# An attention and FFN layer on one core: the first pair's weights are split twice and kept in the second row, and a multiply moves to GpSimd

## The chip, the core and the metric

The kernel runs on one core of a Trainium2 chip. A core has five engines that run side by side, each with its own queue of instructions in a fixed order: TensorE (PE, matmuls; its weight loads are listed as PEld), VectorE (DVE), ScalarE (ACT), GpSimd (POOL) and SyncE (SP, which here issues nearly all DMAs). An instruction waits at the head of its queue until what it needs is there, and everything behind it in that queue waits too. The metric is the device time of one execution in microseconds. Of the kernel before, three runs took 1340.47, 1340.90 and 1341.65 us; the median is 1340.9.

## The reference

The input is four sequences (rows of the batch, "rows" below) of 512 tokens with 512 features. One attention layer with 16 heads and one low-rank mixture FFN, each with a residual and a LayerNorm:

```python
q, k = heads(x @ Wq, 64), heads(x @ Wk, 64)
v = heads(x @ Wv, 128)
s = clip(heads(x @ Ws, 64), -32, 32)
z = cumlogsumexp(s, axis=time)
g, p = exp(z[t-1] - z[t]), exp(s - z)
hk = hk * g[:, None] + k[:, None] * p[None, :]      # for each step t
ok = q @ hk                                          # q scaled by 64 ** -0.5
pv = softmax(ok)
hv = hv * g[:, None] + p[:, None] * v[None, :]
ov = pv @ hv
o = ov * rsqrt(mean(ov ** 2) + 1e-5) * g_norm_weight
o = o * silu(x @ Wg)
x = layernorm(x + o @ Wo)
h = relu(x @ W1 + b1)
alpha = softmax(h @ W2 + b2)                         # 8 experts
x = layernorm(x + sum_k alpha[k] * U[k] @ (V[k] @ x))
```

## The kernel before

**Precision.** All matmuls take operands in a rounded 32-bit format (F32R). To keep float32 accuracy every operand is split into a high part (a copy that rounds) and a low part (the original minus the high part), and a product is three matmuls: high by high, high by low, low by high. So every weight and every activation costs one copy and one subtraction before PE can use it.

**Tiling.** Two heads make a pair; a row has eight pairs, p = 0 to 7, and a unit of work is one pair of one row, 32 in all. For each unit the steps are: `decay` (ps_s, and from it et, the running sum cum, its reciprocal rc, and est), `key` and `query` (ps_k, ps_q), `gates` (ps_g, gate), `value` (ps_v, vh, vl), two causal score steps over `attend` (PE writes pa; ACT copies it to `at`, DVE subtracts and adds, POOL masks it with an affine select), `sum_keys` (po_k), `soft` (a softmax of twelve small steps on DVE, ACT and POOL, which ends in wst), `sum_values` (po_v), `norm` and `combine` (po_y, added by DVE to the row's tile y). After its eight pairs a row goes through LayerNorm, the FFN (ps_h, pt_lg, ps_vx, po_f) and the second LayerNorm, between the attention units of the row that follows.

**The order.** A recording layer (`InOrder`) chains all instructions of all engines in program order, so each engine's queue holds its instructions in exactly the order in which the program calls them. That order comes from a long string, `PLAN`, written by a planner: a letter takes the next step of its kind and issues its PE work (s decay, k key, q query, g gates, v value, c and d the two score steps, x and y the two sums, o soft, n norm, w combine, b and f a weight fetch, and so on). A step leaves its work for other engines behind in small pieces, one list for each letter and engine. A mark and a letter issue the next such piece: `^` ACT, `.` DVE, `,` POOL, `;` SP; a number between them skips pieces. `SLOTS` are strings of digits, also from the planner, that say which of the buffers wt0 to wt6, wraw0 to wraw5, tmp0 to tmp6 and pa0 to pa3 each new tile takes.

**Weights.** `fetch(key, on)` brings one weight tile of 128x512. Its key is the matrix and the pair, with a half for g, v and o: a pair has nine (s, k, q, two g, two v, two o). The first fetch of a key, in the first row (letter b), loads the raw tile from DRAM into a `wraw` buffer, makes the high and the low part in a `wt` buffer, and stores both parts (512 KB) to a scratch tensor in DRAM, `kept_...`. Each later fetch of the key (letter f) reads that tensor in one DMA. High and low part are made by ACT and DVE; for pair 0 and the matrices s, k, q, g and v POOL makes both (`early`).

**The norm.** `norm(u, h, on)` takes one head. PE multiplies the split squares by a matrix of 1/128 (pt_ms); ACT computes Ln and Exp, which gives `rstd`, the reciprocal norm; DVE multiplies the gated value t1 by it in place (in the profile `t<-t,rstd`); ACT makes the high part oh and POOL the low part ol, and `combine` multiplies both by Wo. There are 64 of these.

Of the kernel before, what the change touches and what calls it, by code (L numbers as in the profile page):

```python
# [18 lines left out]
def tile_abc_attention_ffn(  # L19
# [22 lines left out]
    class InOrder:  # L42
# [41 lines left out]
        lpoooooooommoooooooooooooooooooooooorrrr,p,pbbbblbbl^l.ll^l.ll^l,b.l^l,b.ls,b;bb,1b^b,b.b^bq,b;bb.s  # L84
        ;1b.b^sb,b;bb.sek^q;b,sb.q^s,b^see.s^ke,s;b^kb^e.suuk^u^b,b.k,1b.e,b.ui.b^1k^i^i,b;bb.i.i;bb^i,ic^c
        ^c.c.1c^c;b,b.cb^k.c.cu,c^cs.k^b;p,c.c,b.c.b,c;bxb.cxx^b.s;b,cxbx.bx^sxxx.s,se;bxgb^s,s^x^s.x.sxx^ge
        ug.s^x^g.x^u,x^g.u^b.ge^g.oq^b.b^g.o;b^gb.b^o.g;bb.o^q.pv,o^b.q.b^oev^e.o;bb.e^oi^v.ov^i,o.v^i.i.i.o
        ^it,i^t.ov^t.t^o.t.o^bd^v.b^b.v;b^db.b^dg^d.d;b^d.1db.d.d,d.d,d.1d.dy^g.d,d^b,dy^g.by^g;b^yyb.g^yv
        ^1y.y^y.y.1yc,y.1y^c^c.y,y^cv.c^c.1c.yv^v.c.c,c.c,c.1cnxv.c^n.c,c.v^n,cx^b.nxxx^vx.bxxx^nx.vx;bx^xg
        ,nb^x.x^b.x.b,x;bsb^b.o.b.o;bb^o.s^s.ov,o^b.b,s^oeeee;bv.o^eb,s^o.et^v.o^t,o.v^t^g.tk.t^g.o^g.s.o^s  # L90
        .g^o^s.od^k.s^k^b.s^d.k^dq.d^d^d.1d.d.d,d.d,d.1d.du.du,d^qy.b^u,dy^b.q;byb^y.u.b^yy;b.yi^ybs.y^y^i,y
        .1y^i.1y.y.iv.i^b.s^i.b,i^sc;b.s,sb^c^c.c^sk.1c,s^c.c^s.c.c^c,c.s,c.cv.s^k,c^k.c^b.kxe^bxex.c^vux.b
        ,cxexx.vx^x;bnxb.b^n,yxxxt.x^n;bb.y^xv^t.n^t.x^nuq.t^u,x.t.u,n.o.oew^q^o.qw^e.o.w,o.ew^o.w.og^o.w.o
        ,o.op^gwb.o^p^g.pv^o.w;p^g.o^b.gd^v.b^b.v^d;b^db.dg^d.1d^d.d^b.d,d.d,d.1d.d.d,di.b^gy,d^i^g.by;bb^i
        ^gy.i;b^y.iy.gb^i^y,ink^1y.y^y.y^n.1y,y^n.1y.yc^1k.n^c^n.c^ks.c,nl^c.k^c.c^c,c.1c.c.c,c.cp,c.sxvb^p
        .c^b.p,c^sl.b;p^b,st.s;b^lbx,sv^t^t.l^su.tx^vx.tnx.b^sx,ynx^n.vx;bexbv.y^n.s^x.nxxxv.s^n.x^x,n.xp^vu
        vb,x^p.v^u.p^bv.o^b;p^b.u.o^be.bq^v^o.b;bb.v^b;b.ob^b.b,ow.b;b^qb^oeg.q;bb.o.w^o.b^b.o;bewb.b^e,o.b
        ;b^bbg^n.o^g;bb.e^n^g.o.n^gw^o.w^g.gw^g.o^n.w^g.wd,n.g^d^d.d^d.1ds^d.d.d,d.d,d.1d.d.d,d.bi,d^iy.s^i
        ;bby.i^s.it^i.s,s^1yy^t^t.ty^s.t,i^yg,s^s.y^y.s^y.y.s,y.1yc^g.y^c^g.yk^c.c^g.1c^c.c^c.g,c.c.c,cx.1cp
        ^k.cx^kb.c,c^p.kuex^b,cx.pxx^bee.bx;px^xxx.bv^b;bb.x^b;b^b.bbxxn^b.bv;b,y^xb.b;b^nbg^n.y;bb^v.x.n,x  # L100
        .v^n.bq^g,n^g.o;bb^g.o.g^ow^q.o,o.qw.w^o.onu.we^ow^u.o^e.uv,o^n.w.e^nn.ov^1n.n^1n.op^v.nwb^o.v^p.o^n
        .p^n,n.wd;p^b^d.b,n^dk^d.d;b^d.1db^b.d.d,d^b.d^b,d.1d.di.d^1k,dy.b^i^i,dy.i;b.i^ib.by^y,i.by;b^ybs.y
        ;b^yb.y^y.1y,y.1y.y,yc.s^c.y^s.c^kg.s,s^c^c^c.k^s,s.c.c^s.1cq^g.s,c^g.c^g.s,c.c.cp,c^q.gepb^px.cebx
        ^px.q,cxx^bx.pxex^xnx.p;px^bxux.x^nt.b^xl^n.b;bgb^t.x^t;p^l.n,x^b;b.t.t^b.lb^b.bw^g.o^b;bb^g.bw.o^b
        ;bb^g.wu^on.bw.g^u;bb.o.w,ov.u.w^ov.b^b.o;bb.b^ow.b;b^vb.o^ng;b.v,ob^b.w^n,n.o^n.b^bs.o^g;bb.n^g.b^o
        ^n.o;bb^ge,nw.s^e.g^s.e^b.s.wd^d^d,s^s.d^d,s.1dg^s.d.d^d.s,d.d.s,d.di.d^g,dy.b^i^gy.d;b^i,d^g.iyb.i
        ^i.gy^y,i^yv^1y.y^y.y.1yc,y.1y^c^c.y,y^cq.c^c.1c.y.c.c,c.c,cp.1c^qv.cb^p.c,c.q^b,c.p^bxxx.bx^v;pexx
        ^bx.bxxe^xx.vxx;b^bl;b.xn^xbee.b^lbw.x^n;bb.l^e,xfk^n.w.n.o.el.o^kfg.b^k^o.k;bb^l.o,o.lv^o^b.o.bu^ou
        t;b^u.ovb^t.u^t,o^g.t.t^gi.ow^v.o^g.v^i^ow.g^i.o^nf.i,n^b.i.w^i.wd^d^d,i.d^d^d.1ds.d.d,d.d,d.1d.d.d
        ,d.b,dy^b.s;byb.b^st^1y;b.s,sy^t^ty.t^s.t,sk^y^s.y^y.s^y.y.s,y^1kf.1yc^c.y^c.y^kg^c.c^c.k.c.c,c.1c.c  # L110
        v.c^gf,c.c^g,c.ce,ce^gxxxn.gxx^nx,yxxex^x.yxn^nxx.xev^x.n^e.x^nqf.e^v,xf.v,n.o.on^qwf^o.qu.ov.w,o^ow
        .o^ow.w.ou,oq.w^u^n.u.o^2n^n.o^1n.n^ow.nf.o^nf.wd^nf,n^d^d.d,n^d.1dv^d.d.d,d.d,di.1d^vy.d^i.d,d^i.v
        ,dy.i.i^iy,i^y^yy.ys^y.y^y,y.1y.1y.y,yc^b.s^c.y^s.c^ck.s,s^q^c^c.q^s,s.c.c^s.1cg^k.s,c^k^b.c.s,c.c.c
        xt,c^gf.k^txe^g.cxx.b,cxv^t^g.t;b.t.bux.gx;bx^xxnx.xx^nexv^x^n.xef.ne^vv,xf^e.v.ew.o.ow.w^o.ouv.w,o
        ^u.u^og^v.o.v^o.o,ov^gf^g.oi^g.ow^i.g^i^o.i.iw.o^i,i.w^nf.wdf,n^d^d.d^d.1ds^d.d.d,d.d,d.1d.d.d,dy,d
        .sfy^st^1y.s,s^ty^t.tv^s.t,s^y^s.yy^b.sk^v.y^y.s^y,y.v^b.y.yc^1kf.y^c.b^c^k.cg;b^c.1c^c.k.c.c,c.c,c
        .1cv^gf.c.c,c^g.b,cx^gxux;bee.gnxx^nu,yxxxe^ux.y^nxxx.uv^x.n^x.x^ne.xg^v,n^e.v.e,xw.o^gf.o^gv^o.w^g
        .mw.g.o,oi.w^iq^i.m^o.i.o^m^m.m^o.mwf.i^q.o^i.q,om.wm^2m,i.og^2m.m.o^o.3m.ow^gf.3m^gf^g.wdf.g^d^d.m
        ^dv.d^d.d^m.d^m,dg^b.mf^v.m.d.d,d.1d.d.d,dm.v^gfy,d^m.bm^gy.m;b^mn^g.my^y.gy^yk^n.y^y.y^n,y^y.n.y^nf
        .yc^1k,n^c.y^c^ks^c.k^c.c.1c.c.c,c.cnqf,c.1cb.c,y.c.s,c.y,c^s.sxx,s^qexexxt.q^sx,sg^n^s^n.s^t.n^t^x  # L120
        .su^nxefx.th^g.t,n.x^g^g.gxx^hxw^h^b,hex.w^ev^x.b.e;bnhb.x^n,x^n.n.on^hw.o^hf^1n,hw.w^o^1n.nuv^u.w^b
        .o.u,ow.b^v^nfg.v^o;b,nb^n.w.o,n^oh.o^gf,o^g^g.o.gw^hf.o^hw^o.w^b.oi.bm^i^i.w;bw^m,h.i.i^i,i.wd^d^d
        .d^d.1dh^d.d.d,d.d,d.1d.d.d,dy,d^hfm^hy.m,hm^yy.m^yy.ym.y^yk^y.m,y.1y.y.ym^1k,yf.mc.y^c^c^k.cs^m.1c
        ^c.k^c.m.c.c,c.cnqf,c.1c.c.c,c.s,c^s.s,sxx^qxfmv.q^m^s,s.m^nxxv^s^n.s.nmf^vxfee.sx^mumx.v^xxh^1m.xxx
        .mufx^ut^x.ue^mh.x^t.m^t,x.t.t.ogf.m.o^m^o.m.om,of^om.m.om^o.m.ow.m,o^nf.oe^gvf,n^e.w^g.ov^g.e^o.gn
        ^vm.o^n.vf^n.mdf.n^d^d.d^n.1dh^d.d,n^d.d.d.1d,d.d.d,dm,dyf^m,dt.m^ti^my^t.m^iy^i^y.t.ty^y.i.i^ig.y^y
        ,i.y^y.1y,y.1y.y,yc^gf^g.y^c^gs.c^c.g^c.c^c.c,c.1c.cx.cm,cf.ch,c.s.c^s,c.s,sxxfxx^sexx,s^mxk^s.m^x.s
        ^m.x.sn.m^kxfxxv^k^n.k^nux.nee^xm.x,xn.mmm^1n.1m^1n.oeg^e.n.o.m^o.eu.omf^u,o.m.u^ow.2m^m^m.ov.m^o.m
        ;m.w;mmmmmf.o^vf.1m,o^gf.v^gwf.o^g.mg.o.g^o.w.ow.m^gf^gw^m.w^g^mf.g^nf^n.wd,n.m^d^d,n^dq.d^d;m.1d.d
        .d,d.d,d.1d.dy.d,d^qf.mi,d.q^iy;m^i.iy.i^y^iy^y,is^1y.y^y.y.1y,y.1yl.y,yc.s^c.y^s.cf^ck,s.s^c^c,s.c  # L130
        ^s.c.1c^svf.c,c^k.s^k,c.cv.s,c.cn.k^vxxex.c^nux.vx,cex^nxxxx^xx.next^x.x^te.xu^tq^e.t,x.t^u.e.u.o.ov
        ^qf^o.qi.o,o^iw^i.i.i^i^o,iw.w.ow^o.w.ow.w,o^nf.onvf,n^n.w^n.osf^v.nf^o.v^n.o,nd.sf^s^d.s,s^dg^d^d.d
        ^s.1d,s.d^s.d.d,d.sv^gf,d^g.d.sl,d^gy.d^l.gv.d.l,dy^vy.v^y^yy.yv^y.y^y,y.1yw.1y.y,y.wc.y^c^c.c^ck.1c
        ^c.c.c,c.c,c.1c.c.c,cxl^kf,cxx^kn^l.kxxux^nx.lxex^xxex^nx.xt^x.ne^ten^t.xq^e.t,x.t.e.o.ow^qf^o.quv.o
        ^u.w,o.ugf^of^v.o.v^o^1n.ow,o^gf^1n.o^gg.n^g.o.g^o.ww.o^gf^gf^n.wdf^n,n^g^d.gg,n^d.d^d^d.1d.d.d,d.d
        ,d.1dl.d^gf.dy,d^ll,d^g.li^ly^g.ly^i.g^i^yy.i^y.is^i.y^y,i.y^y.1y,y.1yw.yf,y.s.yv^s.w,s.s,sc^c^s.ck
        ^c.c^s,c.c^c.s^c.c.s,c.cev^kf.1c^k.c.c,c.kxx,c^vxxxen.vex^nnxxx^xv^n.x^1n.nx^1nxxt^x.n^tuu.xw^t^u.t
        ,x.t.uv.w.owf.o^vf^o.vw.w.o^nf,oeq.w^nf,n^e^o.e.o,n^ogf^q.o,o.q.ow^gf.o^gv^o.w^g.o.gd^d^d.d^d.1ds^d
        .d.d,d.d,d.1d.d.d,dy,d.sfv^s.s,si^vy^i.v^sy,s^i^s.iy.i^i.s^yk,i^y.s^1y.y^y.y.1y,yc^1kf.1y.y^c,y^c.c
        ^kq.1c^c.y^c.k.c.c,c.c,cv.1c^qf.c.c,c.qx,cxnxx^nxexxx^nuxx^xxe.neut^u.x^tx.ug^t^x.t.t.x,xw^gf.o^g.ow  # L140
        ^g.w^o.gv.o.w,osf^of^v.o.v^o.owf,o^nf.ovf,n.w.oev^e.s^o.e^sg.o^v.s.v^s^sdf^g.s^d.s^g,s.dg^d^g.d,s.d
        ^d.g^d,d.d.d,d.1di^gf.dv.d^i,d^g,d^i^g.iy.i^i.gy,iy^y^yy.yv^y.y^y,y.1yfc^vf.1y^c.y^c.v^ck^c.c.1c.c.c
        ,c.c,c.1cn.c^kvf.c,c^k^n,y.kn,c^n.yexxx^1nxux.nx^1nv^x.n^n.xxe^v,nt^t.vxex^tx.txx.tg^x.x,xuw.o^gf^u
        .o^g.uw^o.w^g.mv.g.o.w,ov.m^owf^m.of^v^m.v^onq.m^1n.m.o^1n.w,o.m.om^qfem^2m.og^e.n^o.q^2m.o.3mw.e^gf
        .3m^gf^n.wdf^n,n.m^g^d.gs,n^m^d.d^m.1d^d^d.m.m.d.d,dv.df,d.1d.d.dv,d.s,d^si.s,st^i^i^ty.i^t.i^s.ty,s
# [49 lines left out]
    def f(t):  # L195
# [8 lines left out]
            04152041520415364201543620136541362054120536  # L204
        """,
        "wraw": """
            0123450132450132450132450132450132450132450132450132450132450132450132450132450132450132514032514032
            5140325140325140325140404032
        """,
        "tmp": """  # L210
# [1175 lines left out]
```

## Time and profile before

| | |
|---|---|
| median of three runs | 1340.9 us |
| profiled execution, whole time | 1339.01 us |
| profiled execution, span from the first to the last instruction | 1337.3 us |
| mean granted clock of TensorE | 0.998 |
| PE busy | 1317.9 us, 8706 matmuls |
| DVE, ACT, POOL busy | 1084.5, 847.2, 553.5 us |
| DMA | 212.36 MB, 159 GB/s over the span |

The page comes from one profiled execution. A group's line names the engine, the operation, the tile written and the tiles read (buffer numbers left out), the shape and the count; after the bar stand the busy time in us, the mean duration of one in ns, and the idle time of the engine just before these instructions, with what ended it ("<-DVE at": an instruction of DVE that wrote `at`). PE's matmuls are pipelined: each is shown with a modelled end that overlaps the next. In a timeline the columns are start in us, duration in us, engine, line, operation, tiles, shapes and count, and in brackets the idle time before. L56 is the line of the recording layer through which nearly all instructions pass, so lines of the program can't be told apart by it, and the tiles' names are used.

### The profile page before, as it was taken

The numbers are of one execution on the slowest core, as the hardware profiler recorded it, in microseconds if no ns is written. First come the engines' busy times: TensorE is split into PE (matmuls) and PEld (weight loads), VectorE is DVE, ScalarE is ACT, GpSimd is POOL, SyncE is SP. The second block draws the span as 40 slices with busy tenths as digits, with TensorE's granted clock in tenths as the row PEclk, the third lists the DMA queues.
The fourth block names the chain that finished last, engine by engine and source line by source line (L and its number), as shares of the span: only waits on it lengthen the run. The fifth ranks groups of instructions, "written<-read, shape, count | busy, mean of one in ns | idle before, by whom it ended". The sixth has DMA issues, their size and how long they took to land.

```text
span 1337.3 us, 24043 instructions
## 1 busy us (share of the span) xinstructions
PE 1317.9 (99%) x8706; PEld 1139.0 (85%) x8706; DVE 1084.5 (81%) x2075; ACT 847.2 (63%) x1858; POOL 553.5 (41%) x623
## 2 busy tenths in 40 slices
PE   9999999999999999999999999999999999999997
PEld 7878888888888888888888888888888888888885
DVE  5888999988788778877779678878778887877855
ACT  4767787766676556666566655666666666666632
POOL 8344444444434343534343533334433344453310
PEclk9999999999999999999999999999999999999999
DMA  9555767763444346433344433544444343344452
GB/s 323 181 166 174 260 197 243 251 209 119 156 143 151 127 142 205 162 130 135 98 146 139 170 111 126 188 143 135 150 142 136 101 158 127 117 136 142 143 173 95
DMA packets 94007, 212.36 MB, mean 159 GB/s; under 512 B 12992, under 2 KB 43712, under 8 KB 93888
## 3 DMA queue, kind: packets, MB, share of 16 engines
q1 hardware_dynamic: 93360, 210.56, 46.9%
q8 instruction: 69, 1.13, 0.3%
q14 instruction: 50, 0.41, 0.1%
q10 hardware_dynamic: 528, 0.26, 0.1%
HBM read 162.55 MB, written 48.23 MB: 158 GB/s over the span
## 4 chain that ended last, share of the span: by engine, by line
PE 87%; DVE 7%; ACT 3%; POOL 1%; issue 1%; DMA 0%; SPq 0%; POOLq 0%; ACTq 0%; DVEq 0%
PE po_y L56 12%; PE ps_g L56 12%; PE ps_v L56 12%; PE po_v L56 7%; PE ps_s L56 6%; PE ps_k L56 6%; PE ps_q L56 6%; PE pa L56 5%; PE po_k L56 4%; PE ps_h L56 3%; PE po_f L56 3%; PE ps_vx L56 3%; PE pt_s L56 3%; PE pt_ms L56 1%; DVE at L56 1%
## 5 line engine op out<-in xcount | busy, mean ns | idle before, releaser
L56 POOL TENSOR_SCALAR_AFFINE_SELECT at<-at 128x512 fp32r<-128x512 f32 x256 | 170.8, 689 | 137.2 <-DVE at L56 123.3
L56 PE MATMUL po_y<-wt,oh 128*128 128x512 f32 x512 | 176.2, 396 | 0.1
L56 DVE TENSOR_TENSOR at<-pa,at 128x384 fp32r<-128x384 f32 x256 | 131.5, 549 | 7.4 <-ACT at L56 6.7
L56 POOL TENSOR_TENSOR ol<-t,oh 128x512 fp32r<-128x512 f32 x64 | 85.7, 1347 | 113.4 <-ACT oh L56 112.9
L56 ACT CAST at<-pa 128x384 fp32r<-128x384 f32 x256 | 107.5, 492 | 29.9 <-PE pa L56 28.2
L56 PEld LDWEIGHTS po_y<-wt,oh 128*128 128x128 f32 x512 | 96.3, 188 | 20.2 <-DVE okc L56 0.3
L56 PE MATMUL po_y<-wt,ol 128*128 128x512 f32 x256 | 100.2, 391 | 0.2 <-POOL ol L56 0.2
L56 DVE TENSOR_TENSOR y<-y,po_y 128x512 f32<-128x512 f32 x128 | 86.8, 680 | 11.6 <-PE po_y L56 10.7
L56 POOL TENSOR_SCALAR sqs<-sq 64x512 fp32r<-64x512 f32 x64 | 50.0, 781 | 95.1 <-DVE sq L56 84.0
L56 PE MATMUL po_v<-at,vh 128*128 128x256 f32 (+1 forms) x512 | 87.4, 278 | 0.0
L56 POOL TENSOR_TENSOR okc<-okc,rc 128x512 f32<-128x512 f32 x32 | 43.8, 1370 | 98.6 <-DVE okc L56 98.6
L56 PE MATMUL po_k<-at,ee 128*128 128x256 f32 (+3 forms) x512 | 82.9, 287 | 0.9 <-POOL at L56 0.8
L56 ACT ACTIVATE sq<-po_v 64x512 f32<-64x512 f32 x128 | 75.1, 591 | 9.5 <-PE po_v L56 7.5
L56 PEld LDWEIGHTS po_v<-at,vh 128*128 128x128 f32 x512 | 77.9, 190 | 0.9
L56 ACT ACTIVATE sg<-ps_g 128x512 f32<-128x512 f32 x64 | 38.2, 597 | 60.7 <-PE ps_g L56 55.7
L56 PEld LDWEIGHTS po_k<-at,ee 128*128 128x128 f32 (+1 forms) x512 | 69.0, 163 | 5.8 <-POOL at L56 2.1
L56 POOL TENSOR_TENSOR pr<-pr,mx 128x512 f32<-128x512 f32 x32 | 34.0, 1062 | 90.3 <-DVE mx L56 89.9
L56 POOL TENSOR_TENSOR pr<-pr,ss 128x512 f32<-128x512 f32 x32 | 33.9, 1059 | 88.5 <-DVE ss L56 62.4
L56 PE MATMUL po_v<-at,vl 128*128 128x256 f32 (+1 forms) x256 | 69.9, 273 | 0.3 <-POOL at L56 0.3
L56 DVE TENSOR_TENSOR at<-at,pa 128x128 fp32r<-128x128 f32 x256 | 62.8, 279 | 0.4
L56 DVE TENSOR_TENSOR t<-po_v,gate 128x512 f32<-128x512 f32 x64 | 44.1, 689 | 20.9 <-ACT sq L56 18.0
L56 POOL TENSOR_SCALAR est<-et 128x512 fp32r<-128x512 f32 x32 | 39.0, 1218 | 52.3 <-PE pa L56 23.7
(303 smaller groups left out, 3873.5 us busy)
## 6 DMA issues: line engine op xcount, KB each, us to landing
wt<-kept_v SPq DMA_DIRECT2D x48, 512.0 KB, 3.7
wt<-kept_g SPq DMA_DIRECT2D x48, 512.0 KB, 3.4
wt<-kept_o SPq DMA_DIRECT2D x48, 512.0 KB, 3.7
wt<-kept_s SPq DMA_DIRECT2D x24, 512.0 KB, 4.0
wt<-kept_k SPq DMA_DIRECT2D x24, 512.0 KB, 3.8
wt<-kept_q SPq DMA_DIRECT2D x24, 512.0 KB, 3.7
kept_g<-wt SPq DMA_DIRECT2D x16, 512.0 KB, 5.5
kept_v<-wt SPq DMA_DIRECT2D x16, 512.0 KB, 4.1
```

The costliest lines, as they stand in the source:

```text
L56: ins = fn(*args, **kwargs)
```

## The change

There are two changes, and a new `PLAN` and new `SLOTS` that order the whole program with them.

First, the nine keys of pair 0 (`key[1] == 0`, matrices s, k, q, g, v, o) are not kept in the first row: the split is made and used, and nothing is stored. In the second row the raw tile is loaded again and split again, then by ACT and DVE, and stored; the third and fourth rows read the kept tensor. All these second fetches count as first ones (letter b) in the lists that `PLAN` draws from. The DMA that loads a raw tile goes through ACT's queue for the very first fetch and through SP's for all others, as before; the test is on the new set `seen`.

Second, the multiply by the reciprocal norm is issued on POOL and not on DVE.

```diff
+    seen = set()
...
-        (SP if kept else ACT).dma_start(raw.rearrange("p (a b) -> p a b", a=a), src)
-        kept[key] = dpool.tile([P, 2, 512], F32, name="kept_" + "_".join(map(str, key)))
-        early = nm in "skqgv" and p0 == 0
+        (SP if seen else ACT).dma_start(raw.rearrange("p (a b) -> p a b", a=a), src)
+
+        again = key not in seen and key[1] == 0 and nm in "skqgvo"
+        seen.add(key)
+        if not again:
+            kept[key] = dpool.tile([P, 2, 512], F32, name="kept_" + "_".join(map(str, key)))
+        early = nm in "skqgv" and p0 == 0 and again
...
             (POOL if early else DVE).tensor_sub(wt[:, 1, :], raw, f(wt[:, 0, :]))
 
+        if again:
+            return
+
         @on("s")
         def _():
             SP.dma_start(kept[key], f(got[0]))
...
-        @on("d")
-        def _():
-            DVE.tensor_mul(t1, t1, j.pop("rstd"))
+        @on("p")
+        def _():
+            POOL.tensor_mul(t1, t1, j.pop("rstd"))
...
-    first = list(dict.fromkeys(key for key in wanted if key[0] not in "VU"))
-    later = list(wanted)
-    for key in first:
-        later.remove(key)
+    first, later = [], []
+    for i, key in enumerate(wanted):
+        n = wanted[:i].count(key) - (key[1] == 0 and key[0] in "skqgvo")
+        (first if n < 1 and key[0] not in "VU" else later).append(key)
```

The first two lines of the old `PLAN` and of the new one:

```diff
-        lpoooooooommoooooooooooooooooooooooorrrr,p,pbbbblbbl^l.ll^l.ll^l,b.l^l,b.ls,b;bb,1b^b,b.b^bq,b;bb.s
-        ;1b.b^sb,b;bb.sek^q;b,sb.q^s,b^see.s^ke,s;b^kb^e.suuk^u^b,b.k,1b.e,b.ui.b^1k^i^i,b;bb.i.i;bb^i,ic^c
...
+        lpoooooooommoooooooooooooooooooooooorrrr,p,pbbbbblbl^l.ll^l.ll^l,b.l^l,b.ls,bb,1b^b,b.b^bk,bb.s;bb.b
+        ^s,bb.se;b^kb,s^kuee.ke^suq,b^e^s.e^u,sb.s^bk,b^q.u.s,1b.q,b.bi^1k^i,bb^i.i;b.ib^i,ic^c.c^cb^c.c,b.c
...
```

## The prediction

> **What bounds the kernel now.** I read the page's busy shares first, then the busy time by stretch, then what TensorE (PE) waited for, then the rows of the instructions that the change moves.
>
> ```profile
> PE 1317.9 (99%) x8706; PEld 1139.0 (85%) x8706; DVE 1084.5 (81%) x2075; ACT 847.2 (63%) x1858; POOL 553.5 (41%) x623
> ...
> PE 87%; DVE 7%; ACT 3%; POOL 1%; issue 1%; DMA 0%; SPq 0%; POOLq 0%; ACTq 0%; DVEq 0%
> ```
>
> PE is the bound: it is busy for 99% of the span and carries 87% of the chain that ended last. A change that leaves PE's work alone can only win what PE still loses. Where that is, the stretches show (columns: length, then busy us and instructions of PE, PEld, DVE, ACT, POOL, then clock, DMA share, GB/s):
>
> ```profile
> 9.20:30.00 20.80, 18.93 (x103) 15.40 (x104) 15.26 (x26) 10.16 (x23) 18.03 (x18) 1.00 1.05 359
> 30.00:60.00 30.00, 28.99 (x217) 25.25 (x215) 25.07 (x48) 23.03 (x52) 9.86 (x13) 1.00 0.71 239
> 60.00:100.00 40.00, 37.02 (x259) 31.91 (x259) 35.08 (x68) 26.14 (x58) 18.83 (x20) 1.00 0.43 138
> 100.00:150.00 50.00, 50.00 (x367) 45.04 (x366) 45.52 (x85) 38.13 (x85) 23.03 (x25) 1.00 0.53 182
> 150.00:250.00 100.00, 99.11 (x639) 84.09 (x638) 94.52 (x176) 78.87 (x168) 46.19 (x47) 1.00 0.76 256
> 250.00:350.00 100.00, 99.52 (x703) 86.57 (x703) 84.75 (x167) 67.60 (x152) 42.81 (x48) 1.00 0.48 164
> ```
>
> PE idles 1.87, 1.01, 2.98, 0, 0.89 and 0.48 us: 7.2 us between 9.2 and 350 us, and from there to 1300 us the same view has only 1.5 us more. The other 11 us of idle time are the start and the tail, which the change does not touch. From 30 us on VectorE (DVE) is at 84 to 95% in these stretches: in the first row it splits weights besides its usual work. PE's waits from 9.2 to 100 us name it:
>
> ```profile
> PE pt_k L56 <- DVE at L56: 0.9, 1, 0.9
> PE ps_k L56 <- DVE vl L56: 0.9, 1, 0.9
> PE ps_v L56 <- DVE et L56: 0.8, 1, 0.8
> PE pt_k L56 <- ACT kf L56: 0.6, 1, 0.6
> ```
>
> **The change part by part.** The instruction orders of the two programs give the counts: PE 8708 in both, DMAs on SP 477 in both, DVE 2077 to 2022 (64 norm multiplies gone, 9 splits more), ACT 1861 to 1870, POOL 628 to 692. PE's matmuls are the same ones; the plan only shuffles them. Distances below are PE's own work between two places of an order, at 0.227 us for a 512-column matmul (ps_s x12 in 2.72 us in the timeline).
>
> ```profile
> L56 DVE TENSOR_TENSOR t<-t,rstd 128x512 f32<-128x512 f32 x64 | 47.9, 753 | 8.9 <-ACT rstd L56 8.1
> L56 POOL TENSOR_TENSOR okc<-okc,rc 128x512 f32<-128x512 f32 x32 | 43.8, 1370 | 98.6 <-DVE okc L56 98.6
> L56 DVE TENSOR_TENSOR wt<-wraw,wt 128x512 fp32r<-128x512 f32 x69 | 52.6, 775 | 3.4 <-ACT wt L56 3.2
> L56 ACT CAST wt<-wraw 128x512 fp32r<-128x512 f32 x69 | 41.5, 624 | 13.3 <-PE ps_s L56 8.5 <-DMA wraw<-in_L_attn_Wk_dram 1.6 <-PE ps_g L56 1.2
> ```
>
> The okc row is the POOL price of the moved multiply: same shape, both inputs in SBUF. So DVE loses 64 x 0.753 = 48.2 us and gains 9 x 0.775 = 7.0, net -41; POOL gains 64 x 1.37 = 87.7; ACT 9 x 0.62 = 5.6.
>
> *1. Nine stores less in the first row.* Pair 0's nine kept tiles (512 KB each) were stored there; seven of those stores stood among the first 30 us, where DMA is at 1.05 of its engines. They move to the second row, and nine 512 KB reads there become 256 KB loads from the weights: the count on SP stays. The loads behind them in SP's queue go out earlier, but only ACT's 1.6 us wait for Wk names a weight there, and none of PE's waits from 9.2 us on does. Bounds -1.6 to 0; I take 0.
>
> *2. The first 30 us.* PE's 0.9 us wait near 25 us (pt_k) is for a PSUM bank that two DVE steps on `at` free. DVE did both heads' 128x384 subtractions first and then the addition; the new order puts the first head's addition right after its subtraction, so one 0.55 us step less lies ahead: -0.55 (bounds -0.9 to 0). Against it, pt_k for pair 0 now has one transposition of pt_e ahead of it where there were three: +0.2 (0 to +0.3).
>
> *3. 60 to 100 us.* DVE's timeline, and below it PE's:
>
> ```profile
> 70.69 0.71 DVE L56 STREAM_TRANSPOSE pr<-okc 128x512 f32<-128x512 f32 x1 [1.18 <-POOL okc L56]
> 71.33 0.65 DVE L56 TENSOR_TENSOR wt<-wraw,wt 128x512 fp32r<-128x512 f32 x1
> 71.90 0.68 DVE L56 TENSOR_REDUCE mx<-pr 128x16 f32<-128x512 f32 x1
> 72.54 0.69 DVE L56 TENSOR_SCALAR et<-ps_s 128x512 f32<-128x512 f32 x1
> ...
> 73.28 0.74 PE L56 MATMUL ps_v<-wt,x_0h 128*128 128x256 f32 x4 [0.78 <-DVE et L56]
> ```
>
> PE waits for et, which queues behind the split of a weight. In the new order that split stands ahead of the transposition, inside the 1.18 us in which DVE waits for POOL anyway: et, and the softmax chain that the next three PE waits hang on, come 0.65 us earlier, once: -0.65. Bounds: 0, if the raw weight is not there that early, to -3.0, all that PE idles in this stretch. The multiply at 64.7 us (1.17 us long) leaves DVE too, but its place is followed by idle time, so I add nothing for it.
>
> *4. 100 to 250 us.* Nine multiplies leave (6.2 us of busy time by the stretches of that tile). One case is plain:
>
> ```profile
> 237.43 0.68 DVE L56 TENSOR_TENSOR t<-t,rstd 128x512 f32<-128x512 f32 x1
> ...
> 242.57 0.67 DVE L56 TENSOR_TENSOR y<-y,po_y 128x512 f32<-128x512 f32 x1
> ...
> 243.29 0.61 PE L56 MATMUL po_v<-wst,s 64*128 64x256 f32 x5 [0.42 <-DVE y L56]
> ```
>
> DVE has no gap from 231.4 us to this addition, and the multiply stands among it: -0.6. PE shows 0.42 us idle, but the matmul before started 0.74 us earlier (at 242.55): a wait shows about 0.3 us short, since the modelled end covers its first part. So the rest of this stretch gets -0.5 (bounds for all of it -1.8, twice PE's idle time, to 0).
>
> *5. The second row.* Nine splits more: seven between about 260 and 320 us, two (Wo) near 400. DVE was at 85% in 250 to 350; it gets 5.4 us and loses 3.4: 87%. POOL's own split of these tiles stays where it was, in the first row. SP's nine stores now wait here for DVE, and reads of later tiles queue behind them; SP is 0% of the chain, and a read lands in 3.4 to 4.0 us. +0.3, bounds 0 to +2.1 (the net).
>
> *6. After 350 us.* DVE goes from about 81 to 77%. PE idles 1.5 us here in all, in some ten waits that show short as above: -0.7, bounds -3 to 0.
>
> *7. The slower multiply.* From the matmul pt_ms to the product's low half the chain was 0.42 + 0.69 + 0.63 + 0.75 + 0.62 + 1.35 = 4.5 us, and becomes 5.1, with handovers some 5.4. PE's own work from pt_ms to the first matmul that reads it is 5.3 in one case of 64 (the last pair of row 3), and 6.9 or more in the others; the median is 29. +0.3. Bounds: 0 to 13 x 0.62 = +8.1, if the thirteen with less than 9 us all lose what the multiply got slower.
>
> *8. POOL's queue.* Behind a multiply that waits for ACT stand the masks (`at`, 0.69 us each), for which PE waits. In the new order 2 of 256 masks come directly after a multiply. PE's present waits for masks are 0.8 us in all. +0.5, bounds 0 to +5 (some eight masks late by half of 1.37).
>
> Sum: -0.55 + 0.2 - 0.65 - 0.6 - 0.5 + 0.3 - 0.7 + 0.3 + 0.5 = -1.7. The profiled execution took 1339.0 us (span 1337.3 and 1.7 around it), 1.9 under the median, so I predict 1340.9 - 1.7 = **1339.2**.
>
> **A rule against it.** The multiply reads two SBUF tiles, and its row in the tile's view is uneven: minimum 648, median 692, maximum 1796 ns. The Trainium skill (SBUF — State Buffer, Who interferes with whom) says why that could follow the work to POOL: a DVE instruction with two SBUF inputs contends with a GpSimd instruction that reads SBUF, and the loser blocks for the whole instruction. By it each POOL multiply could hold up a split, sqs, sq, rc, cum, w or wst on DVE: 21 such starts fall into 87.7 us (325 over the span), at half of 1.37 us some 15 us on DVE, an estimate by that page; DVE's net gain would be 26, not 41, and the sum about -0.8. By the rows the excess of the mean over the median was 64 x 0.06 = 4 us, and goes away with the instruction.
>
> **The rivals.**
> A. *DVE's relief counts in full.* For it: DVE at 84 to 95% wherever PE idles. Against: one of the 64 multiplies lies before 100 us and four before 150, where most of the idle time is. If half of the 7.2 us of idle time goes, and half of some 4 us that show short, that is -5.6; with the +1.1 of terms 5, 7 and 8, -4.5: 1336.4.
> B. *POOL becomes the late engine* (slower than before). Place: the norm chain and the masks behind it. Price 0.62 us for each norm whose cover runs out, 0.7 for a mask. The time is level with before from 1.7 us of such losses beyond mine, three norms or masks; with six norms and three masks it is -1.7 + 3.7 + 2.1 = +4.1: 1345.0. For it: POOL goes from 41 to 48%, and its multiply is nearly twice as long. Against: 62 of 64 multiplies have no mask behind them.
> C. *The second row starves.* A load of raw weights (4.3 us to land) and 1.4 us of splitting take the place of a read (3.4). Two waits of 1.5 us: +3 beyond mine, 1342.2; three, 1343.7. Against: Ws and Wk are split 9 and 14 us of PE's work ahead of their first use, and DVE has 13% free there.
>
> **How the numbers follow.** A measurement tells about 0.2% (2.7 us) from no change. Chances: my forecast 0.45, A 0.29, B 0.18, C 0.08. The forecast's own spread (terms 2 to 8) is 1336.5 to 1342.5; a fifth of it lies below 1338.2 and almost none above 1343.6. Faster: 0.09 + 0.29 = 0.38. Slower: B's 0.18, 0.05 of C and 0.01 of the forecast, 0.24. Within 0.2%: 0.38. The range 1333.5 to 1346 reaches from A with all of the 7.2 us won to B with a mask or norm more; beyond lie about 0.1 on either side.
>
> **What would show it.** DVE busy near 1043 us, POOL near 641, ACT near 853; t<-t,rstd on POOL at about 1.37 us; PE idle from 60 to 100 us down from 3.0 to about 2.3; pt_k near 25 us waiting under half a microsecond; DMA from 9 to 30 us clearly under 1.05. I am wrong if PE waits for POOL `at`, `ol` or ACT `oh` by more than 3 us in all, if PE idles over 1 us more in 250 to 350 us, or if PE idles 2 us less before 60 us, which would mean that DMA, not DVE, held the start.

## The result, and the profile after

| | before | after |
|---|---|---|
| median, first comparison (5 runs each) | 1340.47 us | 1345.22 us |
| ratio, 95% interval | | 1.0040 [1.0029, 1.0051] |
| median, second comparison (19 and 5 runs) | 1339.59 us | 1346.42 us |
| ratio, 95% interval | | 1.0050 [1.0037, 1.0062] |
| profiled execution (span) | 1339.01 (1337.3) us | 1344.7 (1343.0) us |

The changed kernel is slower by 0.4 to 0.5%. The forecast was 1339.2 us, no clear change.

The busy shares and the chain that ended last, from the page of the changed kernel:

```profile
PE 1319.3 (98%) x8706; PEld 1138.6 (85%) x8706; DVE 1061.8 (79%) x2020; ACT 854.9 (64%) x1867; POOL 637.8 (47%) x687
...
PE 77%; DVE 10%; ACT 6%; POOL 3%; issue 2%; DMA 1%; SPq 0%; POOLq 0%; ACTq 0%; DVEq 0%
```

POOL and ACT are where they were expected (641 and 853 us). DVE is not: 1043 us was forecast, 1061.8 came, so 19 of the 41 us that should have left DVE are still there. PE's part of the chain fell from 87 to 77%, and DVE, ACT and POOL took its place.

Busy time by stretch, changed kernel (length, then busy us and instructions of PE, PEld, DVE, ACT, POOL, then clock, DMA share, GB/s):

```profile
9.20:30.00 20.80, 19.04 (x110) 15.67 (x109) 16.13 (x26) 10.68 (x23) 19.09 (x19) 1.00 0.80 243
30.00:60.00 30.00, 29.34 (x223) 25.84 (x222) 25.32 (x50) 23.64 (x52) 9.89 (x12) 1.00 0.59 195
60.00:100.00 40.00, 36.98 (x268) 32.00 (x266) 34.92 (x68) 27.60 (x60) 21.51 (x23) 1.00 0.38 126
100.00:150.00 50.00, 49.76 (x347) 43.85 (x346) 44.47 (x80) 36.89 (x82) 24.72 (x26) 1.00 0.53 179
150.00:250.00 100.00, 98.05 (x637) 83.45 (x635) 91.38 (x167) 77.58 (x166) 53.48 (x53) 1.00 0.73 248
250.00:350.00 100.00, 96.42 (x664) 83.57 (x663) 85.14 (x161) 68.43 (x153) 48.37 (x49) 1.00 0.52 178
```

PE idles 1.95 us from 150 to 250 us (0.89 before) and 3.58 us from 250 to 350 us (0.48 before). That second stretch is where row 1 ends and row 2 begins. PE's waits in 236 to 350 us name what it waited for; first those of the kernel before, then those of the changed one:

```profile
PE po_v L56 <- DVE y L56: 0.6, 2, 0.4
PE po_y L56 <- POOL ol L56: 0.2, 1, 0.2
PE po_v L56 <- POOL at L56: 0.2, 1, 0.2
```

```profile
PE po_k L56 <- POOL at L56: 0.9, 1, 0.9
PE po_v L56 <- DVE y L56: 0.8, 1, 0.8
PE pa L56 <- DVE sf L56: 0.6, 1, 0.6
PE po_k L56 <- DVE t L56: 0.6, 1, 0.6
PE po_y L56 <- POOL ol L56: 0.6, 1, 0.6
PE pa L56 <- DVE wst L56: 0.5, 1, 0.5
...
```

DVE stands behind 2.5 us of the lines shown of the changed kernel and POOL behind 1.5. The rows of the moved multiply and of the splits say why DVE kept so much of its time (the last line is from the kernel before):

```profile
L56 POOL TENSOR_TENSOR t<-t,rstd 128x512 f32<-128x512 f32 x64 | 85.3, 1336 | 60.4 <-ACT rstd L56 57.8 <-PE pt_s L56 2.3
...
L56 DVE TENSOR_TENSOR wt<-wraw,wt 128x512 fp32r<-128x512 f32 x78 | 63.5, 827 | 6.6 <-ACT wt L56 6.4
...
L56 DVE TENSOR_TENSOR w<-w,rc 128x512 f32<-128x512 f32 x32 | 29.6, 926 | 0.7
```

```profile
L56 DVE TENSOR_TENSOR w<-w,rc 128x512 f32<-128x512 f32 x32 | 22.5, 703 | 0.5
```

The multiply took what its neighbour had promised (1.34 us against 1.37). But the softmax's `w<-w,rc` takes 926 ns in the mean where it took 703 before, and the splits 827 where they took 775. One case, from the changed kernel's timeline of DVE and then of POOL:

```profile
796.62 0.71 DVE L56 STREAM_TRANSPOSE w<-pr 128x512 f32<-128x512 f32 x1 [0.39 <-POOL pr L56]
797.37 1.78 DVE L56 TENSOR_TENSOR w<-w,rc 128x512 f32<-128x512 f32 x1
799.83 0.69 DVE L56 TENSOR_TENSOR wst<-w,wst 128x512 fp32r<-128x512 f32 x1 [0.68 <-ACT wst L56]
```

```profile
797.30 1.29 POOL L56 TENSOR_TENSOR t<-t,rstd 128x512 f32<-128x512 f32 x1 [0.72 <-ACT rstd L56]
```

POOL started 0.07 us earlier, and DVE's instruction of 0.69 us ended 0.56 us after POOL's did: nearly as if it had begun its work only then. PE waited 1.03 us there for ACT's part of wst.

How much of this there is in all can be read from the trace. Take for each DVE instruction what it lasts beyond the lower quartile of its group (same tiles, same shape), count it where it is over 0.15 us, and put it down to the POOL instruction that overlaps it most. Beside `t<-t,rstd` on POOL, 22 DVE instructions are stretched by 14.7 us together. This measure is called "stretch beside the multiply" below.

So there were three suspects: the multiply on POOL (it stretches DVE, it is longer, it fills POOL's queue), the second row's nine extra splits, and the new order itself.

### The profile page after: what moved, and what is told of

Read it like the earlier page. It is cut to its first block, busy times and chain, and to the rows that moved or that the text cites. A ratio compares the mean times of both kernels' runs of the same rounds, so it can differ in the third digit from the quotient of the medians.

```text
span 1343.0 us, 24022 instructions
## 1 busy us (share of the span) xinstructions
PE 1319.3 (98%) x8706; PEld 1138.6 (85%) x8706; DVE 1061.8 (79%) x2020; ACT 854.9 (64%) x1867; POOL 637.8 (47%) x687
## 4 chain that ended last, share of the span: by engine, by line
PE 77%; DVE 10%; ACT 6%; POOL 3%; issue 2%; DMA 1%; SPq 0%; POOLq 0%; ACTq 0%; DVEq 0%
PE ps_g L56 11%; PE ps_v L56 10%; PE po_y L56 10%; PE po_v L56 7%; PE ps_s L56 6%; PE pa L56 5%; PE ps_k L56 5%; PE ps_q L56 5%; PE po_k L56 4%; PE ps_h L56 3%; PE ps_vx L56 3%; PE po_f L56 3%; PE pt_s L56 2%; DVE at L56 1%; DVE wt L56 1%
## 5 line engine op out<-in xcount | busy, mean ns | idle before, releaser
L56 POOL TENSOR_SCALAR_AFFINE_SELECT at<-at 128x512 fp32r<-128x512 f32 x256 | 173.7, 701 | 119.9 <-DVE at L56 105.5
L56 POOL TENSOR_TENSOR t<-t,rstd 128x512 f32<-128x512 f32 x64 | 85.3, 1336 | 60.4 <-ACT rstd L56 57.8
L56 DVE TENSOR_TENSOR wt<-wraw,wt 128x512 fp32r<-128x512 f32 x78 | 63.5, 827 | 6.6 <-ACT wt L56 6.4
```

The lines of the kernel that those rows point to most:

```text
L56: ins = fn(*args, **kwargs)
```

## The experiments

Each comparison has its own runs of the kernel before; differences are given against these.

### Taking the parts apart

Theory 1 was the multiply on POOL, theory 2 the second row's splits, theory 3 the order.

**The multiply back on DVE, at its new place.**

```diff
         @on("p")
         def _():
-            POOL.tensor_mul(t1, t1, j.pop("rstd"))
+            DVE.tensor_mul(t1, t1, j.pop("rstd"))
```

> The changed kernel, with only the 64 multiplies by the reciprocal norm back on DVE at the same place of the order. Changed kernel 1345.2 us, kernel before 1340.5. Theory 1 (the multiply on POOL costs the time: its 1.34 us hold up POOL's queue, and while it runs a DVE split of two SBUF inputs takes 1.77 us in place of 0.68): 1339 to 1341.5, PE idle from 250 to 350 us down from 3.6 to under 1.5 us, no split on DVE above 1.2 us there. Theory 2 (the second row's nine splits starve PE): 1344 to 1346.5, idle in 250 to 350 us stays above 3. Theory 3 (the new order itself is worse for PE, whatever the engine): 1344 to 1347, and at 798 us PE still idles over 1 us.

1346.28 us against 1339.95, ratio 1.0051 [1.0039, 1.0064]: no faster than the changed kernel. Theory 1 in its simple form falls: putting the multiply back does not bring the time back.

**The old kernel with the multiply on POOL**, at its old place.

```diff
         @on("d")
         def _():
-            DVE.tensor_mul(t1, t1, j.pop("rstd"))
+            POOL.tensor_mul(t1, t1, j.pop("rstd"))
```

> The kernel before, with only the 64 multiplies on POOL at their old place of the order. Theory 1 (POOL multiply): slower than before by 2 to 6 us, 1342.5 to 1346.5, with DVE splits and w of 1.7 us and longer wherever a POOL multiply runs. Theories 2 and 3: within 1.5 us of before, 1339 to 1342; by DVE's relief alone it could gain up to 3.

1350.24 us, ratio 1.0077 [1.0063, 1.0091]: 10.3 us slower, beyond any theory's figure. DVE's stretch beside the multiply is 20.1 us on 26 instructions. The multiply on POOL is dear in the old order.

**Pair 0 stored in the first row and read back in the second**, in the new order, multiply on POOL.

```diff
+        second = key in seen and key[1] == 0 and nm in "skqgvo"
+        if not second:
             (SP if seen else ACT).dma_start(raw..., src)
...
             got.append(wt)
+            if second:
+                SP.dma_start(f(wt), first_kept[key])     # no copy, no subtraction
...
             (POOL if early else DVE).tensor_sub(wt[:, 1, :], raw, f(wt[:, 0, :]))
+            if again:
+                SP.dma_start(first_kept[key], f(wt))
```

> The changed kernel, but pair 0's nine weights are stored in the first row (right after their subtraction) and read back in the second (one read at the place of ACT's copy; no raw load, no second split). The multiply stays on POOL. Theory 1: 1343.5 to 1345.5, at most one of the stalls near 295 and 314 us gone. Theory 2 (second row's splits): 1340 to 1342, PE idle in 250 to 350 us under 1.5. Theory 3: 1344.5 to 1346. The start can lose up to 1.5 us of its gain, as the stores stand among the first loads again.

1344.61 us, ratio 1.0035 [1.0023, 1.0048]: +4.7 where the whole change has +4.75 and +6.8. Theory 2 falls as the main cause: the second comparison leaves it up to 2.2 us, the first 0.1. PE's two losses of 1.17 us near 295 and 314 us, counted from the start of one matmul to that of the next beyond the usual step, are both gone (theory 1 had allowed one).

**Both parts undone, only the order left.** The edit of the first run and that of the third together:

```diff
-            POOL.tensor_mul(t1, t1, j.pop("rstd"))
+            DVE.tensor_mul(t1, t1, j.pop("rstd"))
...
+            if second:
+                SP.dma_start(f(wt), first_kept[key])
```

> Both parts undone in the new order: multiply on DVE, pair 0 stored in the first row and read back in the second. What is left of the change is the order alone. Theory 1: as with the multiply alone on DVE, 1339 to 1341.5. Theory 2: 1340 to 1342. If both parts cost: 1336 to 1339, since the start keeps some of the 2.3 us that it wins by 67 us. Theory 3 (the order): 1343.5 or more, with PE idle over 1 us at 798 us.

1344.14 us, ratio 1.0032 [1.0020, 1.0045]. The kernels with one part undone are 4.7 and 6.3 us slower than before, and the order with neither part still has 4.2 of it. This spoke for theory 3, though with the multiply on DVE.

### Mending the order by hand

In the trace with only the order, three of PE's largest new losses, of 0.92 us each by the same count, lie near 242, 253 and 277 us, and the changed kernel has the same. Three local edits of `PLAN` should remove them:

```diff
 near 241 us
-i ^g w ^i .g ^i ;b b .s .i ^s .i .w d
+i ^g w ^i ^i .i .i .g ;b b .s ^s .w d
 near 253 us
-c ^c ^c .1y ^c ^c .y v
+v c ^c ^c .1y ^c ^c .y
 near 276 us
-.w .o ^g n .o ^v w ^n .g ^o .v ^n .o ^b
+.o ^g n .o ^v w ^n ^o .w ^n .o .g .v ^b
```

> The changed kernel with three places of its order put right and nothing else: near 241 us DVE adds sf (which frees the PSUM bank PE waits for) before the gate and et; near 253 us twelve matmuls of ps_v go ahead of the scores of pair 6, so that DVE can free the bank of po_k meanwhile; near 276 us DVE makes wst before y, gate and vl. PE's extra waits there are 0.96, 0.92 and 1.3 us. If the order is what costs (the run with only the order was 4.2 us slower than before): 1341.5 to 1343, the three waits under 0.4 us each. If these waits are only where a delay from elsewhere (late weights, late softmax) comes to light: 1344.3 to 1345.5, and PE waits a little later instead.

1348.49 us, ratio 1.0067 [1.0054, 1.0081]: no better than the changed kernel (1.0040 and, in the second comparison, 1.0050 [1.0037, 1.0062], whose interval overlaps), and above both forecasts. PE's waits from 239 to 350 us in this kernel:

```profile
PE po_v L56 <- DVE y L56: 2.1, 3, 0.9
PE po_k L56 <- POOL at L56: 1.6, 3, 0.9
PE po_v L56 <- POOL at L56: 0.8, 2, 0.6
PE po_y L56 <- POOL ol L56: 0.6, 1, 0.6
...
```

The waits for sf and for t are gone, and those for wst fell from 0.8 to 0.6 us. In their place PE waits for y, 2.1 us where it was 0.8. This fits what the edits moved ahead of y on DVE's queue; no run separates it.

The fourth place, where DVE's subtractions and additions on the score tiles are again taken by turns:

```diff
-g ^c .k ^c .c .1c .c .c ,c .c v ^g ,c .1c ^b .c .c ,c ^g x .b x x ,c e x
+g ^c .c ^c .k .c .c ,c .1c .c v .c ^g ,c .c ^b ,c .c ^g e ,c x x x .b x
```

> As the run with three places, and a fourth: near 294 us DVE subtracts and adds on the score tiles by turns, as in the old order, so that POOL's masks are spread out ahead of the second row's splits (PE waited 1.17 us for a mask there, and the wait was there in both runs that have the second splits, in neither that reads kept tiles). Order theory: 0.7 to 1.2 us less than with three places. If the splits themselves hold DVE up: within 0.4 us of it.

1346.83 us, ratio 1.0058 [1.0046, 1.0071]. PE's 1.17 us loss to a mask near 295 us is gone, and the time is 1.7 us under the run with three places, a step that the intervals only suggest.

The same three edits in the kernel with only the order (multiply on DVE, pair 0 kept in the first row):

> The run with the order alone (multiply on DVE, pair 0 kept in the first row, 1344.1 us) with the three places put right. Order theory: 1341 to 1342.2, so that about half to three quarters of what the order costs lies at these three places. If a delay from elsewhere: 1343.5 to 1344.5.

1346.70 us, ratio 1.0052 [1.0040, 1.0065] against 1.0032 [1.0020, 1.0045] without the edits: not faster, rather slower. Taking one engine's piece forward seems only to have chosen which of several was late. Theory 3 as "three bad places" falls.

### What the multiply costs in each order

**POOL busier, chain no longer.** The kernel before, with products that nobody needs behind each ol:

```diff
             POOL.tensor_sub(ol, t1, f(u["o", h][0]))
+            for x in (slice(0, 256), slice(256, 512)):
+                POOL.tensor_mul(junk, t1[:, x], t1[:, x])
```

> The kernel before with 64 extra products of the multiply's size on GpSimd (two of 128x256 each, t1 by t1 into a tile that nobody reads), right after each ol. DVE keeps its multiply, and nothing waits for the extra products, so the norm chain is not longer; what they add is 87 us of POOL reading SBUF and a longer POOL queue. The kernel before with the multiply moved to POOL was 10.3 us slower. Theory L (POOL's reads hold up DVE's two-input instructions): 1344 to 1352, DVE instructions stretched by 15 us or more in all, beyond the 34 us of before. Theory C (the 0.6 us longer chain from pt_ms to ol is what cost 10.3 us): 1339 to 1342.

1371.21 us, ratio 1.0238 [1.0224, 1.0252]: +31.6. But the reason is not the one that theory L gave. DVE is stretched by 44 us in all (counted from the lower quartile, without the floor of 0.15 us), 10 more than before and not 15. PE's waits in this kernel show part of the cause:

```profile
PE po_v L56 <- POOL at L56: 11.6, 13, 2.0
PE po_y L56 <- POOL ol L56: 3.1, 3, 1.4
```

po_v waited 11.6 us for masks, 0.3 us before: they stood behind the useless products in POOL's queue. With the waits of po_k for masks and of po_y for ol it is 16.8 us against 1.3; what made up the rest of the 31.6 us, PE's waits do not name. So the run says that POOL's queue is a price of its own, and nothing clear on the reads.

**The multiplies left out**, first in the kernel before, then in the new order with pair 0 kept in the first row. In both, this line goes (the multiplies are then missing from the output; in the new order the edit is shown against the kernel with only the order):

```diff
-            DVE.tensor_mul(t1, t1, j.pop("rstd"))
+            j.pop("rstd")
```

> The kernel before with the 64 multiplies left out (the output is not scaled by the reciprocal norm); ACT still makes rstd, and oh still queues behind it. This is the most that DVE's relief can give in the old order: 48 us of DVE. If the old order is bound by DVE where PE waits: 1334 to 1338. If PE's waits there are latencies that DVE's total doesn't move: 1338.5 to 1340.5.

> The new order with pair 0 kept in the first row and read back in the second, and the 64 multiplies left out: the order alone with the multiply for free (with it on DVE: 1344.1, on POOL: 1344.6). If the order's loss is DVE's load at the wrong moments: 1337 to 1341. If it is the order in which PE meets its operands, whatever DVE carries: 1342 to 1344.

1335.91 us, ratio 0.9974 [0.9964, 0.9983], and 1336.69 us, 0.9982 [0.9973, 0.9991]. Without the multiply the two orders differ by 0.8 us, which the intervals do not tell apart. The new order is not worse in itself: it has 2.9 us less than the kernel before when the multiply is free, and 4.2 us more when DVE has to do it. So in the new order the multiply on DVE costs 7.1 us, in the old one 3.7. One reading is that the new order leaves DVE less room where the old order has the multiply; but on POOL, too, the multiply costs 7.6 us in the new order (4.7 plus 2.9), and no run takes that further. The waits near 242, 253 and 277 us don't come from the multiply: PE waits 0.6 us for sf, 0.6 for t and 0.5 for DVE's wst there with it on DVE and without it.

**The changed kernel again**, unedited, on the same chip as these:

> The changed kernel as it is, beside the others on one chip: 1344.5 to 1346, by its first comparison. If the first 30 us of its profile were a lucky start (it reached the third ps_s at 67.2 us, other runs with the same first instructions at 69.7 and 70.4 us): the profiled run is up to 3 us longer than the shortest run here.

1346.42 us, +6.8. Its profiled run was its shortest, so nothing here says that the first profile had a lucky start.

### Why POOL's multiply costs so much

Two properties of the multiply on POOL could be at fault: it reads two SBUF tiles for 1.3 us (theory L), or it lasts 1.3 us where DVE's lasts 0.7, with the norm chain and POOL's queue behind it (theory C). A stand-in separates them: the same place, the same waits, about the same time on POOL, but fills in place of reads. The multiply is missing from it, and t1 is all ones behind it.

```diff
-            POOL.tensor_mul(t1, t1, j.pop("rstd"))
+            POOL.tensor_mul(t1[:, 0:16], t1[:, 0:16], j.pop("rstd")[:, 0:16])
+            for n in (512, 512, 160):
+                POOL.memset(t1[:, 0:n], 1.0)
```

> The changed kernel with each multiply on GpSimd replaced by a product of 16 columns and three fills of t1 (512, 512 and 160 columns with 1.0; the output is wrong by that): about the same 1.3 us on GpSimd at the same place, the same waits before and behind it, but nearly nothing read from SBUF. Theory L (GpSimd's reads hold DVE up): 1339 to 1342.5, and the 14.7 us by which DVE's instructions were stretched beside t<-t,rstd are gone. Theory C (a longer chain and queue): 1344 to 1346.5, as the changed kernel.

> The same replacement in the old order with the multiply on GpSimd (1350.2 us with the real multiply). Theory L: 1338 to 1344. Theory C: 1348 to 1351.

1350.66 us, 1.0082 [1.0068, 1.0096], and 1350.32 us, 1.0079 [1.0065, 1.0093]. Stretch beside the multiply fell from 14.7 to 0.8 us in the new order and from 20.1 to 1.9 in the old, so it is POOL's reads that stretch DVE. The times, though, did not fall. The stand-in had come out too long: 1.73 us from the start of its first instruction to the end of its last in the mean, 0.39 more than the multiply.

**The changed kernel without the multiplies:**

```diff
-            POOL.tensor_mul(t1, t1, j.pop("rstd"))
+            j.pop("rstd")
```

> The changed kernel with the 64 multiplies left out: the new order with the second row's splits (output not scaled by the reciprocal norm). Without the splits, pair 0 kept in the first row, this was 1336.7 us. If the splits cost 0.6 us (their price with the multiply on GpSimd): 1336.5 to 1338. If they cost 2 (their price with it on DVE): 1338.2 to 1339.5.

1338.06 us, ratio 0.9993 [0.9984, 1.0002]. Against the same without the second splits (0.9982 [0.9973, 0.9991]) the splits cost some 1.8 us, though the intervals overlap. The other two pairs of runs give 2.1 us (multiply on DVE) and 0.1 to 2.2 us (on POOL).

**Stand-ins of matched and of shorter time.** In both orders with the second line, in the new order with the third and the fourth:

```diff
-            for n in (512, 512, 160):
+            for n in (512, 352):
...
+            for n in (352,):
...
+            for n in (512, 432):
```

> The changed kernel with the multiply replaced by a product of 16 columns and fills of 512 and 352 columns, about 1.28 us in all (the multiply takes 1.30 at the median). Theory L (GpSimd's reads hold DVE up): 1339 to 1342.5. Theory C (GpSimd's time in the norm chain and in its queue): 1344.5 to 1347, as the changed kernel, though DVE is stretched by 14 us less.

> The same in the old order, where the real multiply on GpSimd took 1350.2 us and the 1.68 us stand-in 1350.3. Theory L: 1338 to 1344. Theory C: 1346 to 1350.

> The changed kernel with a product of 16 columns and one fill of 352 columns, about 0.7 us in all, what the multiply takes on DVE. Theory C: 1337.5 to 1341, close to the 1338.1 us of the changed kernel without the multiplies, so that the 0.6 us by which GpSimd is slower carry nearly all of the price. Theory L says the same for this run, since little is read; if neither holds, and it is the step to another engine (the handover and the queue behind it) that costs: 1342 or more.

> The changed kernel with a product of 16 columns and fills of 512 and 432 columns in place of the multiply, about 1.33 us in all (the real multiply: 1.34 in the mean, 1.30 at the median), and the output wrong by that. If the reads carry the difference to the changed kernel (1345.2 to 1346.4): 1341.5 to 1343. If it was the 0.09 us: 1343.8 to 1346.5, so that duration alone explains the whole loss in this order.

| stand-in, mean time on POOL from first start to last end | new order | old order |
|---|---|---|
| multiply left out | 1338.06, 0.9993 [0.9984, 1.0002] | 1335.91, 0.9974 [0.9964, 0.9983] |
| 0.72 us, fills | 1338.19, 0.9994 [0.9985, 1.0003] | |
| 1.30 and 1.31 us, fills | 1341.90, 1.0023 [1.0013, 1.0033] | 1342.84, 1.0026 [1.0015, 1.0037] |
| 1.36 us, fills | 1343.13, 1.0028 [1.0018, 1.0039] | |
| 1.73 us, fills | 1350.66, 1.0082 [1.0068, 1.0096] | 1350.32, 1.0079 [1.0065, 1.0093] |
| the multiply, 1.34 us | 1345.22 and 1346.42, 1.0040 [1.0029, 1.0051] and 1.0050 [1.0037, 1.0062] | 1350.24, 1.0077 [1.0063, 1.0091] |

Three things follow. First, handing the step to POOL costs nothing that these runs can tell: at 0.72 us the time is that without any multiply. Second, the duration costs: from 0.72 to 1.36 us the new order loses 5.0 us (+4.1 less -1.0 against their kernels before). It gets steeper beyond: from 1.36 to 1.73 us another 7.4. Third, the reads cost as well. In the old order the multiply is 6.6 us dearer than fills of 1.31 us; the 0.03 us that it is longer is worth some 0.5 of it (by the 7.5 us from 1.31 to 1.73), so some 6 us are left for the reads. In the new order 0.7 to 2.8 us are left, though these fills are 0.03 us longer than the multiply; there the intervals overlap.

Where the 5.0 us fall can be read from the two traces. PE's waits for POOL with fills of 0.72 us, where it never waits for ol, and then of 1.36 us:

```profile
PE po_k L56 <- POOL at L56: 1.4, 2, 1.0
...
PE po_v L56 <- POOL at L56: 0.8, 3, 0.4
```

```profile
PE po_k L56 <- POOL at L56: 1.7, 3, 1.0
...
PE po_y L56 <- POOL ol L56: 1.1, 2, 0.6
...
PE po_v L56 <- POOL at L56: 1.0, 3, 0.4
```

PE's order is the same in both, so its matmuls can be matched one by one, start against start. The second profiled run falls back by 5.6 us. Of these 1.45 come where PE waits for ol, the norm's own product, at two norms (near 241 us and, in the last pair of row 3, near 1277 us); 0.9 at three masks; 1.2 at four waits for DVE's y, t and wst, by then late too. The other 2 us lie where PE shows no wait for POOL or DVE; what made them stays open, and two profiles of the changed kernel differ by 0.6 us in this count.

The same place as above, in the run with fills of 1.36 us, DVE and then POOL:

```profile
795.96 0.71 DVE L56 STREAM_TRANSPOSE w<-pr 128x512 f32<-128x512 f32 x1 [0.39 <-POOL pr L56]
796.71 0.70 DVE L56 TENSOR_TENSOR w<-w,rc 128x512 f32<-128x512 f32 x1
798.10 0.69 DVE L56 TENSOR_TENSOR wst<-w,wst 128x512 fp32r<-128x512 f32 x1 [0.69 <-ACT wst L56]
```

```profile
796.65 0.22 POOL L56 TENSOR_TENSOR t<-t,rstd 128x16 f32<-128x16 f32 x1 [0.72 <-ACT rstd L56]
796.93 1.04 POOL L56 MEMSET t<- 128x512 f32 x2
798.93 1.29 POOL L56 TENSOR_TENSOR ol<-t,oh 128x512 fp32r<-128x512 f32 x1 [0.96 <-ACT oh L56]
```

POOL is busy beside `w<-w,rc` for as long as before, but writes, and DVE takes 0.70 us, not 1.78. PE's wait of 1.03 us at this place is not there either.

## Why the prediction was wrong

Against their kernels before, the runs with the multiply left out, on DVE and on POOL took, in us:

| multiply | old order | new order, pair 0 kept in the first row | new order, second splits |
|---|---|---|---|
| left out | -3.7 | -2.9 | -1.1 |
| on DVE | 0 | +4.2 | +6.3 |
| on POOL | +10.3 | +4.7 | +4.75 and +6.8 (the change) |

The change leads from "on DVE" in the first column to "on POOL" in the last. How the loss divides depends on the way taken. Without the multiply the order costs 0.8 us and the second splits 1.8; the multiply then costs 5.9 to 8.0 on POOL where it cost 3.7 on DVE. With the multiply on DVE the order alone costs 4.2, and moving the multiply within the new order changes little (+0.5 with pair 0 kept, -1.6 to +0.5 with the second splits). Each way adds up to the measured loss, as it must, since it goes through the same runs; so the sums prove neither way. What the runs do show is that with fills of 0.72 us in the multiply's place on POOL the changed kernel is level with the one before (-1.0 us, 0.9994 [0.9985, 1.0003]): on POOL the loss hangs on the multiply's length and its reads.

*Term 7, the slower multiply* (+0.3). This is the step that failed. It counted one norm of 64 whose cover of PE's work, 5.3 us, is as short as the chain, 5.4 us, and gave all others a price of zero. Measured in the new order, 0.65 us more on POOL costs 5.0 us. That one norm does lose, near 1277 us, but so does one near 241 us to which it had given cover of 6.9 us or more, and together these two are only 1.45 of the 5.0. The chain was added up as if each of its instructions started when its input was there. But they stand in queues with a fixed order: masks behind the multiply are late by 0.9 us, and DVE's y, t and wst by 1.2. The bound of +8.1 (13 norms at 0.62) held; the value was taken by counting cover, and cover says nothing on what else waits. That the queues carry the delay to these places is read from the waits; no run separates it.

*Terms 1 to 6, the rest.* They came near by luck. For all of the change but the multiply's engine, terms 1, 2, 3 and 5 had set -0.7 us; with the multiply on DVE it measured +6.3. The price of the new order itself had no term: it was given its gains alone. For taking the multiply off DVE, terms 4 and 6 had set -1.8; from there to fills of 0.72 us on POOL it measured -7.3. In the old order leaving the multiply out wins 3.7, so that even there -1.8 was too small, and rival A's -5.6 as far off on the other side. Two errors of 7.0 and 5.5 us, of opposite sign, nearly cancel: together these terms had set -2.5 and measured -1.0. Why a multiply on DVE costs about twice as much in the new order stays open.

*Term 8, POOL's queue* (+0.5). PE's waits for masks are 2.3 us after (1.7 for po_k, 0.6 for po_v) and 1.1 before (0.8 and 0.3; the prediction's 0.8 left out po_v). So 1.2 us came by name, over twice the value and well inside the bounds of 0 to 5. The run with useless products shows what nearly the same time on POOL, 88.6 us, costs when it stands in front of masks: 31.6 us.

*The rule against it.* The row was weighed too lightly. The prediction priced the stretch at 0.9 us and set it aside because the excess of 4 us on the old multiply "goes away with the instruction". By the estimate from the Trainium skill (SBUF — State Buffer, Who interferes with whom), some 15 us would lie on DVE; the trace has 14.7 us, 22 instructions at 0.67. The page also says that such an instruction of DVE contends with a GpSimd instruction that reads SBUF, not with one that only writes it, and the fills agree: 0.8 us. What the reads cost in time is some 6 us in the old order and 0.7 to 2.8 in the new.

*Term 5, the second row* (+0.3, bounds 0 to 2.1). Near the upper bound, 1.8 (0.1 to 2.2). One wait is plain: PE's loss near 295 us to a mask behind DVE's work on score tiles, with the second splits beside it; it is in the changed kernel and in the one with the multiply on DVE, and in neither of the two that read kept tiles there.

*Term 3, 60 to 100 us* (-0.65). Nothing came: PE idles 3.02 us there, 2.98 before. The split did go ahead of the transposition. DVE's timeline after, and POOL's:

```profile
66.60 0.69 DVE L56 TENSOR_TENSOR wt<-wraw,wt 128x512 fp32r<-128x512 f32 x1
68.08 0.91 DVE L56 TENSOR_TENSOR wt<-wraw,wt 128x512 fp32r<-128x512 f32 x1 [0.79 <-ACT wt L56]
68.91 0.70 DVE L56 STREAM_TRANSPOSE pr<-okc 128x512 f32<-128x512 f32 x1
69.64 0.69 DVE L56 TENSOR_REDUCE mx<-pr 128x16 f32<-128x512 f32 x1
70.25 0.68 DVE L56 TENSOR_SCALAR et<-ps_s 128x512 f32<-128x512 f32 x1
```

```profile
66.65 1.79 POOL L56 TENSOR_TENSOR okc<-okc,rc 128x512 f32<-128x512 f32 x1
68.40 1.74 POOL L56 TENSOR_TENSOR ol<-t,oh 128x512 fp32r<-128x512 f32 x1
```

okc ended at 68.44, but the transposition began at 68.91: the split before it waited for ACT until 68.08 and then ran for 0.91 us beside POOL's okc and ol. So 0.47 us of the gain were lost again. POOL's okc, too, took 1.79 us beside a split, before as after, where its mean is 1.37 and 1.33.

*Terms 1 and 2, the start.* The wait for pt_k went from 0.9 to 0.6 us (-0.55 had been taken), and DMA in 9 to 30 us from 1.05 to 0.80. PE idles 0.46 us less from 9.2 to 60 us, not the 2 us that would have pointed to DMA. Whether the stores' removal helps stays open: the first ps_s came between 8.3 and 9.8 us in runs of kernels with the same first instructions, and this spread is larger than the effect.

*The rivals.* B, "POOL becomes the late engine", was given 0.18 and 1345.0 us; the time is 1345.2. The number is met by luck, since it rests on the same terms 1 to 6; its mechanism was half right: the multiply's length has the price that B gave it, but through two norms, three masks and what DVE then did late, not through six norms and three masks. C had 0.08 and 1342 to 1344; its mechanism gave 1.8 us. Of the signs that would prove the forecast wrong, two came: PE waits for POOL's at and ol 3.3 us in all (over 3), and idles 3.1 us more in 250 to 350 us (over 1).

## What to carry to other kernels

Moving an elementwise step from one loaded engine to a slower one is not priced by the busy time it frees alone, but also by its longer time in the chain and in the new engine's queue: here taking 48 us off DVE was worth 3.7 us in the old order and 7.1 to 7.5 in the new, and 0.65 us more for each of 64 steps took back 5. Before such a move, run the kernel with the step left out and with a stand-in of the new length: the first gives the most that can be won, the second what the length takes back. An order planned for one placement of a step should be compared with that step left out of both orders; otherwise the order is blamed for what the step costs in it.

## What the runs showed of the hardware

- A POOL instruction of 1.3 us that reads SBUF holds up a DVE instruction with two SBUF inputs for nearly its whole length (1.78 us where it takes 0.70). One that fills SBUF for as long does not (0.70 us). The other way too: okc on POOL took 1.79 us beside a DVE split, 1.33 in the mean.
- The time is far from linear in a small step's length: in the new order 64 steps on POOL cost nothing measurable at 0.72 us, and against that 5.0 us at 1.36 and 12.4 at 1.73.
- Three hand edits, each of which removed the wait it was aimed at or made it smaller, left the kernel 2 to 4 us slower in the medians, with intervals that partly overlap.
